# A selective scan on VectorE: an empty instruction ahead of each unit's input product takes over the scan's waits for ScalarE and GpSimd

## The chip, the cores and the metric

The kernel runs on one core of one Trainium2 chip. The metric is the device time of one execution in microseconds, and a kernel is judged by the median over its runs. All times in this document come from such runs, or from a hardware profile of one execution.

## The reference, cut to what matters

The reference is two layers, each a layer norm with a mixing block and a feed-forward block added to the residual, for 4 sequences of 256 tokens with 512 features. The change lies in the mixing block of the second layer, a selective state space scan over 1024 channels with 16 states each:

```
def step(h, inp):
    x_t, dt_t, B_t, C_t = inp
    dA = jnp.exp(dt_t[..., None] * A)
    dBx = dt_t[..., None] * B_t[:, None, :] * x_t[..., None]
    h = dA * h + dBx
    y = jnp.einsum('bdn,bn->bd', h, C_t)
    return (h, y)
...
y = (ys + D_param[None, :, None] * xc) * jax.nn.silu(z)
return jnp.einsum('bdl,hd->blh', y, out_proj_w)
```

For each channel and state there is a decay `dA`, an input product `dBx`, a recurrence over 256 time steps, and a weighted sum of the 16 states by `C`. Around it stand the input projections (`x` and `z`), a causal convolution, the small projections that give `dt`, `B` and `C`, the gate, the output projection, and a routed feed-forward block with 8 experts.

## The kernel before, in words

The first 330 us of the execution hold the first layer (attention and gated feed-forward), in which TensorE works nearly all the time. The rest is the second layer, and it is a chain of 128 **units**. A unit `u` is one sequence `b` (4), one group `c` of 128 channels (8), and one group `g` of 4 states (4): `b, c, g = u // 32, u % 32 // 4, u % 4`. Its tile is 128 partitions by 4 x 256 elements: 32 channels on each quarter of the partitions crossed with the states, and four pieces of 256 time steps side by side.

Every unit passes over four engines:

- **Decays (ScalarE, `decays`, L980).** Four exponentials of `dt * A` into one of three buffers `decay[(u - 4) % 3]`. The loop issues the decays of unit `u + 2` at the head of unit `u`, and the buffer is the one that the scan of unit `u - 1` reads, so the decays of `u + 2` wait for the scan of `u - 1`.
- **Input product (VectorE, `scan_in`, L986).** `bx = B * (dt * x)`. `dus` comes by DMA (four transfers, one for each partition quarter) for each group of four units. `bx` is one PSUM buffer, so the product of a unit waits for the scan of the unit before.
- **Scan (VectorE, `scan`, L1001).** `h = decay * h + bx` as one scan instruction over 1024 elements. `h` has two buffers, so the scan of unit `u` may not overwrite what GpSimd's product of unit `u - 2` still reads. The scan therefore waits for three engines: VectorE itself (`bx`), ScalarE (the decays of `u`) and GpSimd (`hc` of `u - 2`).
- **Weighting and sum (GpSimd L1006, TensorE L1018).** `hc = C * h` on GpSimd into one of three buffers, then four small matmuls add the states up in `ysum`.

The order of the work is written out by hand: lists of calls by unit number (`put`, `put_mid`, `put_late`, `put_end`) place the projections, convolutions, transposes, routing, gates and loads of the next sequence between the units. Each engine executes its instructions in that order. GpSimd has other work between its `hc` products (`step_out` L914 to L918, `step_x` L925, the gate L1026, the convolution's sums L811), and so does ScalarE (activations of the step sizes, table loads at L954 and L708, copies). VectorE has `bx`, the scan, and few other instructions: layer norm statistics (L720, L721, L729), the norm of the small projection (`pp_norm`, L845, issued between `bx` and the scan of one unit per sequence) and the routing (L1053 to L1085).

In the built program an instruction holds one wait of its own; what it must wait for besides stands in front of it as EventSemaphore instructions that hold up to two waits each. Before the change, an EventSemaphore with the waits for VectorE and ScalarE stands between `bx` and the scan, and the scan itself holds the wait for GpSimd. Where the wait for ScalarE is not needed, the EventSemaphore holds the one for VectorE alone. `bx` holds a wait for VectorE, with two EventSemaphores for the DMAs ahead of it in every fourth unit.

Of the kernel before, what the change touches and what calls it, by code (L numbers as in the profile page):

```python
# [11 lines left out]
AF = mybir.ActivationFunctionType  # L12
# [16 lines left out]
NG = 4  # L29
# [12 lines left out]
def block_kernel(  # L42
# [24 lines left out]
    nc = tc.nc  # L67
# [51 lines left out]
    live = {}  # L119
# [536 lines left out]
    xcs, nrms, dts, szs, crows = {}, {}, {}, {}, {}  # L656
# [15 lines left out]
    aneg = w1.tile([P, DC, NG, NU], F32, name="aneg")  # L672
# [15 lines left out]
        pads.append(t)  # L688

    decay = []  # L690

    def decay_tile(pool):
        t = pool.tile([P, NG, S], F32, name=f"decay{len(decay)}")
        nc.gpsimd.memset(t[:, :, 0:1], 0.0)
        decay.append(t)
# [268 lines left out]
    def lend(n, u):  # L964
        tag = lent[n][u]
        pool, bufs = (we, 3) if tag == "w_in" else (w1, 1)
        return pool.tile([P, NG, S], F32, tag=tag, name=n, bufs=bufs)

    def decays(u):
        b, c, g = u // PER, u % PER // NU, u % NU  # L970
        if u >= len(lent["d"]):
            da = decay[(u - 4) % 3]
        elif lent["d"][u] == "d":
            da = decay[0]
        else:
            da = lend("d", u)
            nc.gpsimd.memset(da[:, :, 0:1], 0.0)
        live["da", u] = da
        for k in range(NG):
            nc.scalar.activation(da[:, k, 1:], live["dts", b, c][:, k, 1:], AF.Exp,  # L980
                                 scale=aneg[:, c, k, g : g + 1])

    def scan_in(u):
        b, c, g = u // PER, u % PER // NU, u % NU
        bx = psx.tile([P, NG, S], F32, tag="bx", name="bx")
        nc.vector.tensor_tensor(  # L986
            bx, brow[g // 2][:, g % 2, :].unsqueeze(1).to_broadcast([P, NG, S]), live["dus", b, c], ALU.mult
        )
        live["bx"] = bx

    def scan(u, parts=1):
        b, c, g = u // PER, u % PER // NU, u % NU
        da, bx = live.pop(("da", u)), live["bx"]
        if u < len(lent["h"]):
            h, hc = lend("h", u), lend("hc", u)
        else:
            h = act.tile([P, NG, S], F32, tag="h", name="h", bufs=2)
            hc = act.tile([P, NG, S], F32, tag="hc", name="hc", bufs=3)
        for k in range(parts):
            n = slice(k * NG // parts, (k + 1) * NG // parts)  # L1000
            nc.vector.tensor_tensor_scan(  # L1001
                h[:, n].rearrange("p n t -> p (n t)"), da[:, n].rearrange("p n t -> p (n t)"),
                bx[:, n].rearrange("p n t -> p (n t)"), 0.0, ALU.mult, ALU.add,
            )

            (nc.vector if k == NG - 1 else nc.gpsimd).tensor_tensor(  # L1006
                hc[:, n], h[:, n],
                crows[b][:, g, :].unsqueeze(1).to_broadcast([P, NG // parts, S]), ALU.mult,
            )
        live["hc", u] = hc  # L1010
# [138 lines left out]
    for i in range(2):  # L1149
        v = vec[:, 6 + i, :]  # L1150
        nc.scalar.activation(px[:, i, :], px[:, i, :], AF.Identity, bias=v[:, V_CB : V_CB + 1],
                             scale=v[:, V_CW + KC - 1 : V_CW + KC])
# [33 lines left out]
    u, e, lw = live["u"], live["e"], live["lw"]  # L1186
# [21 lines left out]
    for n, t in (("dt", dt[:, 1, :]), ("du", du[:, 1, :])):  # L1208
        live[n, 0, 0] = scr.tile([2, P, S], F32, tag=n, name=f"{n}d")
        nc.sync.dma_start(live[n, 0, 0][1], t)  # L1210
    decays(0)
    scan_in(0)
    spread("dt", 0, 1)
    spread("du", 0, 1)
    b_rows(0, 1)
    c_rows(0, 1)
    decays(1)
    one_step(2)

# [157 lines left out]
    for u in range(total + 2):  # L1377
# [5 lines left out]
        if 3 <= u < total - 2:  # L1383
            decays(u + 2)
        for f, a in at.get(u, ()):
            f(*a)
        if u < total:
            if u:
                scan_in(u)
            for f, a in mid_at.get(u, ()):  # L1390
                f(*a)
        if shut == (0, 0):
            take_sum(0, 0)
        if u > total:
            b, c = shut
# [3 lines left out]
        if u < total:  # L1399
            scan(u, 1 if u < total - 1 else 4)  # L1400
            if u < 3:
                decays(u + 2)
# [11 lines left out]
        if late and u >= total - PER + 22:  # L1414
            c = late.pop(0)
# [115 lines left out]
```

## Time and profile before

| What | Value |
|---|---|
| Runs (three) | 840.86, 839.10, 839.61 us |
| Median of them | 839.61 us |
| Span of the profiled execution, first to last instruction | 839.1 us |
| VectorE busy | 655.1 us (78% of the span), 604 instructions |
| GpSimd busy | 496.7 us (59%), 389 instructions |
| ScalarE busy | 554.7 us (66%), 1124 instructions |
| TensorE busy | 748.8 us (89%) |
| Mean granted TensorE clock | 0.957 |
| VectorE busy between 466 and 550 us | 79.01 of 84 us |
| VectorE busy between 720 and 831 us | 105.87 of 111 us |

The page gives no time of the profiled execution besides its span; the median of the runs is 0.5 us longer than that span, which is taken as what lies around it.

How to read the profile: PE is TensorE, DVE is VectorE, ACT is ScalarE, POOL is GpSimd, SP issues DMAs. A row of instruction groups gives line, engine, operation, `out<-in` with shapes and the count, then busy time and mean duration of one in ns, then the engine's idle time just before these instructions and what ended it. A row of the timeline gives start and duration in us, and in brackets an idle time of 0.15 us or more ahead of it with the instruction that ended it; shorter gaps are read from the difference of start plus duration and the next start. A row of the waits gives who waited, for whom, the total, how often and the longest. EventSemaphores and empty instructions don't count as busy time.

### The profile page before, as it was taken

Reading aid. Unit: us, or ns where it says so; the run is one execution under the profiler, and the core shown is the slowest. Engines: PE = TensorE matmul, PEld = TensorE weight load, DVE = VectorE, ACT = ScalarE, POOL = GpSimd, SP = SyncE. Lnnn points to the kernel's source line nnn. Section 1 sums busy time; section 2 is a strip of 40 time slices with the busy share of each in tenths; the row PEclk is TensorE's granted clock in tenths of the full one; section 3 lists DMA queues with packets and bytes.
Section 4 is the critical chain, followed back from the end, with each engine's and each line's share of the span. In section 5 each row is a group of like instructions: output and inputs, shape, how many; then the busy total and the mean of one; then the engine's idle time right before and its main releaser. Section 6 shows DMA issues by size and latency. Waiting matters only on the chain.

```text
span 839.1 us, 11113 instructions
## 1 busy us (share of the span) xinstructions
PE 748.8 (89%) x3846; PEld 429.7 (51%) x3846; DVE 655.1 (78%) x604; ACT 554.7 (66%) x1124; POOL 496.7 (59%) x389
## 2 busy tenths in 40 slices
PE   4999999999999999999887899888999987956885
PEld 2665545666555676666543457444457444312331
DVE  4486756288634435798899999989999989999996
ACT  4335564435556277699896898687898786865561
POOL 3133332001343333688869799769699769798764
PEclk9799999999999999999999999989999989998998
DMA  7233332001222332554593554443553343343400
GB/s 226 63 101 105 97 101 62 1 1 38 76 76 80 114 57 64 151 140 125 137 215 114 150 155 125 110 103 117 144 164 114 88 113 111 103 125 102 113 26 25
DMA packets 68642, 86.71 MB, mean 103 GB/s; under 512 B 12221, under 2 KB 52169, under 8 KB 68458
## 3 DMA queue, kind: packets, MB, share of 16 engines
q1 hardware_dynamic: 58794, 65.81, 29.3%
q0 software_dynamic: 9072, 18.35, 7.9%
q10 hardware_dynamic: 720, 1.84, 0.6%
q8 instruction: 30, 0.49, 0.2%
q14 instruction: 26, 0.21, 0.1%
HBM read 66.58 MB, written 10.22 MB: 92 GB/s over the span
## 4 chain that ended last, share of the span: by engine, by line
PE 51%; DVE 25%; ACT 15%; POOL 5%; issue 3%; DMA 1%; DVEq 0%; POOLq 0%; ACTq 0%; SPq 0%
DVE h L1001 15%; ACT decay L980 7%; PE pg L444 6%; PE pu L444 5%; PE po L469 5%; PE px L757 4%; DVE bx L986 4%; POOL hc L1006 4%; PE av L397 4%; PE px L804 4%; PE ysum L1018 3%; PE scT L386 2%; DVE mpl L354 2%; PE pp L831 2%; PE po L1114 2%
## 5 line engine op out<-in xcount | busy, mean ns | idle before, releaser
L1006 POOL TENSOR_TENSOR hc<-h,cr 128x1024 f32<-128x1024 f32 (+1 forms) x130 | 301.7, 2323 | 79.9 <-DVE h L1001 67.5
L1001 DVE TENSOR_TENSOR_SCAN h<-decay,bx 128x1024 f32<-128x1024 f32 (+1 forms) x129 | 288.2, 2236 | 27.0 <-POOL hc L1006 4.7
L980 ACT ACTIVATE decay<-dts,aneg 128x255 f32<-128x255 f32 x504 | 213.4, 501 | 52.3 <-DVE h L1001 42.2
L986 DVE TENSOR_TENSOR bx<-brow,dus 128x1024 f32<-128x1024 f32 x128 | 157.7, 1232 | 5.0 <-DMA dus<-dud 0.6
L1018 PE MATMUL ysum<-hc,stack 128*32 128x256 f32 x1024 | 89.6, 419 | 42.2 <-POOL hc L1006 41.9
L456 POOL TENSOR_TENSOR hlo<-g,hhi 128x512 fp32r<-128x512 f32 x28 | 35.8, 1280 | 115.0 <-ACT hhi L455 115.0
L354 DVE TENSOR_REDUCE mpl<-sc 128x4 f32<-128x1024 f32 x64 | 76.7, 1219 | 22.8 <-PE sc L352 21.3
L427 POOL DMA_DIRECT2D wgu<-in_wgu x56 | 31.1, 555 | 95.9 <-PE pg L444 94.7
L388 ACT ACTIVATE pe<-scT 128x1024 f32<-128x1024 f32 x64 | 64.0, 1023 | 22.9 <-PE sc L352 14.3
L1114 PE MATMUL po<-ow,xc 128*128 128x512 f32 x128 | 69.4, 646 | 4.3 <-POOL xc L1026 3.9
L1018 PEld LDWEIGHTS ysum<-hc,stack 128*32 128x32 f32 x1024 | 21.3, 111 | 100.3 <-POOL hc L1006 70.6
L948 PE MATMUL pz<-xn1T,w_in 128*128 128x256 f32 x256 | 69.4, 420 | 0.0
L948 PEld LDWEIGHTS pz<-xn1T,w_in 128*128 128x128 f32 x256 | 50.8, 208 | 20.7 <-issue 11.9
L757 PE MATMUL px<-xn1T,w_in 128*128 128x256 f32 x256 | 60.9, 383 | 0.4 <-ACT sz L954 0.3
L757 PEld LDWEIGHTS px<-xn1T,w_in 128*128 128x128 f32 x256 | 47.6, 190 | 13.0 <-issue 2.5
L452 DVE SCALAR_TENSOR_TENSOR g<-g,pg 128x512 f32<-128x512 f32 x28 | 19.2, 686 | 43.1 <-ACT g L451 43.1
L444 PE MATMUL pg<-xhi,wgu 128*128 128x512 f32 x112 | 49.6, 443 | 1.0 <-ACT xhi L244 1.0
L469 PE MATMUL po<-wd,hhi 128*128 128x512 f32 x112 | 49.2, 439 | 0.0
L444 PE MATMUL pu<-xhi,wgu 128*128 128x512 f32 x112 | 47.6, 425 | 0.8 <-DVE g L454 0.8
L455 ACT CAST hhi<-g 128x512 fp32r<-128x512 f32 x28 | 17.3, 619 | 45.8 <-DVE g L454 45.8
L444 PE MATMUL pg<-xlo,wgu 128*128 128x512 f32 x112 | 44.9, 401 | 0.7 <-DVE xlo L251 0.7
L444 PE MATMUL pu<-xlo,wgu 128*128 128x512 f32 x112 | 44.5, 397 | 0.0
(237 smaller groups left out, 1276.8 us busy)
## 6 DMA issues: line engine op xcount, KB each, us to landing
dts<-dtd SPq DMA_DIRECT2D x124, 128.0 KB, 2.8
dus<-dud SPq DMA_DIRECT2D x124, 128.0 KB, 3.2
wgu<-in_wgu POOLq DMA_DIRECT2D x56, 256.0 KB, 2.7
w_in<-in_inz SPq DMA_DIRECT2D x16, 512.0 KB, 4.9
w_in<-in_inx SPq DMA_DIRECT2D x14, 512.0 KB, 4.3
dtd<-dt SPq DMA_DIRECT2D x15, 256.0 KB, 2.2
dud<-du SPq DMA_DIRECT2D x15, 256.0 KB, 2.2
wd<-in_wd POOLq DMA_DIRECT2D x7, 512.0 KB, 3.6
```

Of the source, the lines that this page charges most:

```text
L354: nc.vector.tensor_reduce(mpl2[b % 2][:, qb, 2 * hp : 2 * hp + 2, 16 + 2 * gq : 18 + 2 * gq], sc.rearrange("p i (f k) -> p i f k", f=2), A ...
L388: nc.scalar.activation(pes[b, k][:, 2 * t : 2 * t + 2, :], sc, AF.Exp)
L444: mm(ps, lhsT=wgus[i][:, hc, :], rhs=xs[j][:, hc, :], start=(hc == 0 and j == 0), stop=(hc == HC - 1 and j == 1))
L469: mm(po, lhsT=hids[th][j][:, m, i * P : (i + 1) * P], rhs=wd[:, m, :], start=False, stop=(m == MC - 1 and j == 1))
L757: mm(px[:, i, :], lhsT=w[:, i, hc, :], rhs=xns[b][:, hc, :], start=(hc == 0), stop=(hc == HC - 1))
L948: mm(pz[:, i, :], lhsT=w[:, i, hc, :], rhs=xns[b][:, hc, :], start=(hc == 0), stop=(hc == HC - 1))
L980: nc.scalar.activation(da[:, k, 1:], live["dts", b, c][:, k, 1:], AF.Exp, scale=aneg[:, c, k, g : g + 1])
L986: nc.vector.tensor_tensor(bx, brow[g // 2][:, g % 2, :].unsqueeze(1).to_broadcast([P, NG, S]), live["dus", b, c], ALU.mult)
L1001: nc.vector.tensor_tensor_scan(h[:, n].rearrange("p n t -> p (n t)"), da[:, n].rearrange("p n t -> p (n t)"), bx[:, n].rearrange("p n t -> ...
L1006: (nc.vector if k == NG - 1 else nc.gpsimd).tensor_tensor(hc[:, n], h[:, n], crows[b][:, g, :].unsqueeze(1).to_broadcast([P, NG // parts, ...
L1018: mm(ysum[k * NB : (k + 1) * NB, :], lhsT=stack, rhs=hc[:, k, :], start=False, stop=(g == NU - 1))
L1114: mm(live["po", b, i], lhsT=xcs[b][:, c, i * P : (i + 1) * P], rhs=late_w["ow"][:, c, :], start=False, stop=(c == DC - 1))
```

## The change

From unit 8 on, `scan_in` first issues `engine_nop()` on VectorE, and two dependencies are added to it by hand: on the last of the four exponentials of this unit's decays (ScalarE) and on GpSimd's product `hc` of unit `u - 2`. To name them, `decays` and `scan` keep their instructions in a dictionary.

```
+    made = {}
+    early = mybir.DependencyInfo(mybir.DependencyClass.Sync, mybir.DependencyReason.DATA)
...
+            made["da", u] = nc.scalar.activation(
+                da[:, k, 1:], live["dts", b, c][:, k, 1:], AF.Exp, scale=aneg[:, c, k, g : g + 1]
+            )
 
     def scan_in(u):
         b, c, g = u // PER, u % PER // NU, u % NU
+        if u >= 8:
+            i = nc.vector.engine_nop()
+            for n in (("da", u), ("hc", u - 2)):
+                tc.add_manual_dep(i.ins, made[n].ins.name, early, reason="the scan's waits")
         bx = psx.tile([P, NG, S], F32, tag="bx", name="bx")
         nc.vector.tensor_tensor(
...
-            (nc.vector if k == NG - 1 else nc.gpsimd).tensor_tensor(
+            made["hc", u] = (nc.vector if k == NG - 1 else nc.gpsimd).tensor_tensor(
```

In the built program this gives 120 empty instructions. Of a unit from 8 on, VectorE's queue then reads: an EventSemaphore with the wait for ScalarE, the empty instruction with the wait for GpSimd, the EventSemaphores for DMAs in every fourth unit, `bx` with the wait for VectorE, and the scan with the wait for VectorE alone. Nothing else on VectorE moves, and the order of work on the other engines is the same.

Two queues besides VectorE's differ in their waits. On ScalarE, the first exponential of 57 units now also waits for ScalarE's own earlier instruction, so that its wait for the scan stands in an EventSemaphore of its own. On GpSimd, 61 of the `hc` products also wait for GpSimd's own earlier instruction; for these the waits for VectorE and TensorE share one EventSemaphore, where before it held one wait.

More of the change, by code (lines that the diff above doesn't have):

```diff
@@ L979, in decays @@
         for k in range(NG):
-            nc.scalar.activation(da[:, k, 1:], live["dts", b, c][:, k, 1:], AF.Exp,
-                                 scale=aneg[:, c, k, g : g + 1])
+            made["da", u] = nc.scalar.activation(
+                da[:, k, 1:], live["dts", b, c][:, k, 1:], AF.Exp, scale=aneg[:, c, k, g : g + 1]
+            )
     def scan_in(u):
         b, c, g = u // PER, u % PER // NU, u % NU
+        if u >= 8:
+            i = nc.vector.engine_nop()
+            for n in (("da", u), ("hc", u - 2)):
+                tc.add_manual_dep(i.ins, made[n].ins.name, early, reason="the scan's waits")
         bx = psx.tile([P, NG, S], F32, tag="bx", name="bx")
```

## The prediction

> **What bounds the kernel now.** I read the costliest groups of the page first, then the waits, then the timeline of VectorE.
>
> ```profile
> L1006 POOL TENSOR_TENSOR hc<-h,cr 128x1024 f32<-128x1024 f32 (+1 forms) x130 | 301.7, 2323 | 79.9 <-DVE h L1001 67.5
> L1001 DVE TENSOR_TENSOR_SCAN h<-decay,bx 128x1024 f32<-128x1024 f32 (+1 forms) x129 | 288.2, 2236 | 27.0 <-POOL hc L1006 4.7
> L980 ACT ACTIVATE decay<-dts,aneg 128x255 f32<-128x255 f32 x504 | 213.4, 501 | 52.3 <-DVE h L1001 42.2
> L986 DVE TENSOR_TENSOR bx<-brow,dus 128x1024 f32<-128x1024 f32 x128 | 157.7, 1232 | 5.0 <-DMA dus<-dud 0.6
> ```
>
> Scan and product give VectorE 2.29 + 1.23 us in each of 128 units. The scan has 27 us of idle time ahead of it, the product 5; who waits for whom says how little of it is waiting for the other engines.
>
> ```profile
> POOL hc L1006 <- DVE h L1001: 67.5, 50, 5.2
> ACT decay L980 <- DVE h L1001: 42.2, 28, 2.0
> DVE h L1001 <- POOL hc L1006: 4.7, 3, 3.2
> ```
>
> GpSimd and ScalarE wait for VectorE far more than it for them, so VectorE mostly sets the pace, with TensorE taking over in places (the chain that ended last runs through TensorE around 480 to 550 us). VectorE's own rows show what the idle time is:
>
> ```profile
> 805.05 1.23 DVE L986 TENSOR_TENSOR bx<-brow,dus 128x1024 f32<-128x1024 f32 x1
> 806.41 2.29 DVE L1001 TENSOR_TENSOR_SCAN h<-decay,bx 128x1024 f32<-128x1024 f32 x1
> 808.74 1.23 DVE L986 TENSOR_TENSOR bx<-brow,dus 128x1024 f32<-128x1024 f32 x1
> 810.10 2.29 DVE L1001 TENSOR_TENSOR_SCAN h<-decay,bx 128x1024 f32<-128x1024 f32 x1
> ```
>
> From product to scan there is a gap of 806.41 - 805.05 - 1.23 = 0.13 us, from scan to product 808.74 - 806.41 - 2.29 = 0.04. The unrounded medians are 0.132 and 0.035.
>
> **What the change removes.** The scan keeps one wait, and no EventSemaphore stands between product and scan. What remains of the gap is read from other pairs. In the routing, each instruction waits for the one before alone, and reads or writes PSUM as `bx` does:
>
> ```profile
> 433.60 0.20 DVE L1054 TENSOR_TENSOR w<-ex,w 128x32 f32<-128x32 f32 x1
> 433.83 0.20 DVE L1055 TENSOR_TENSOR w<-w,cst 128x32 f32<-128x32 f32 x1
> 473.07 1.23 DVE L986 TENSOR_TENSOR bx<-brow,dus 128x1024 f32<-128x1024 f32 x1
> 474.41 2.29 DVE L1001 TENSOR_TENSOR_SCAN h<-decay,bx 128x1024 f32<-128x1024 f32 x1
> ```
>
> The gap is 0.03 with one wait (first pair), and 0.11 at this scan, whose EventSemaphore holds only VectorE's wait. So it follows the waits, and I take 0.035 for the new scan: 0.097 us less in each of 120 units, 11.6 us gross.
>
> The Trainium skill speaks against this: "VectorE: DVE Perf Modes", section "The DRAIN you can't avoid", says that a semaphore after each VectorE instruction adds nothing, since the next one waits for the pipeline anyway. Here 0.035 and 0.132 differ with the waits, so I go by the rows; by the rule the gap would stay and the sum would be that of the third rival.
>
> **What it adds.** The empty instruction's waits are mostly over while the last scan runs. Does it then take time between scan and product? Not in the trace; the nearest rows are VectorE's smallest instructions without waits:
>
> ```profile
> 0.81 0.06 DVE L87 MEMSET eps<- 128x1 f32 x1 [0.81 <-PEq L1518]
> 0.84 0.06 DVE L88 MEMSET eps<- 128x1 f32 x1
> ```
>
> They follow each other at 0.03 us. An instruction without a wait also starts before the last has ended: the statistics at 463.93 start 0.09 before the scan of 461.73 ends (464.02). Two such steps end before the product could start. Lower end: 0 (not below, as the product still waits for the scan's end). Upper end: as much as the EventSemaphore that went, 0.097. I take 0, by the nearest rows. Where the wait is not over, I count 0.065 from the releaser's end to the product: 0.035 for the hand-over and 0.03 for the step (an estimate from the two rows).
>
> The extra EventSemaphores elsewhere: the first exponential of 57 units starts 0.063 later after the scan (its hand-over from 0.034 to 0.097), the 61 GpSimd products 0.03 later (0.132 less the 0.103 of the one-wait case). Both lie where those engines wait for VectorE; they count only where the engine is then late itself.
>
> **What it moves.** The wait for decays and for `hc` of two units before now holds the product too, and behind it the scan and everything on VectorE. Before, the product (1.23) and the gap (0.13) ran under this wait. Two examples, `bx` of units 58 and 29:
>
> ```profile
> 563.10 1.23 DVE L986 TENSOR_TENSOR bx<-brow,dus 128x1024 f32<-128x1024 f32 x1
> 564.26 1.70 ACT L980 ACTIVATE decay<-dts,aneg 128x255 f32<-128x255 f32 x4
> 566.05 2.29 DVE L1001 TENSOR_TENSOR_SCAN h<-decay,bx 128x1024 f32<-128x1024 f32 x1 [1.72 <-ACT decay L980]
> 451.19 2.34 POOL L1006 TENSOR_TENSOR hc<-h,cr 128x1024 f32<-128x1024 f32 x1
> 452.99 1.23 DVE L986 TENSOR_TENSOR bx<-brow,dus 128x1024 f32<-128x1024 f32 x1
> ```
>
> At 58 the decays end at 565.96, 2.86 after the product started. At 29, `hc` of unit 27 ends at 453.53, 0.54 after. With *late* for this time and *gap* for the old one between product and scan, the scan starts later by (late + 0.065 + 1.232 + 0.035) - (1.232 + gap) = late + 0.10 - gap: 1.24 us at 58, 0.51 at 29. Call it c. I went through all units: the later of the two ends lies after the product's start in 32 of 120.
>
> The gains don't simply pay for this, since a late engine doesn't get earlier with VectorE: its queue has other work (around 453 us, `hc` and step products follow on GpSimd without idle time). So I walk through the units with s, the delay of the scan against before. Each unit lowers s by 0.097; at a late unit s is at least c plus the delay that the late engine itself carries from the scan that last released it (r).
>
> - Unit 10: decays 0.68 late, c 0.65, s 0.65. Units 13 to 19 (383 to 411 us): `hc` late by up to 4.40, old gaps up to 3.20, c at most 1.30, s 1.3. Unit 20: decays, c 1.25, s 1.25.
> - Units 21 to 28: eight gains, and scans that waited for something else anyway (gaps of 0.64 and 0.49): s 0.
> - Unit 29: c 0.51, r 0.2, s 0.7. To unit 42 about -0.1. Units 43 and 47: c 0.12, r 0.25, s 0.4. Unit 51: decays, c 0.61, r 0.3, s 0.9.
> - Unit 53: the norm at L845, between product and scan, waits for ScalarE's root behind TensorE's work (gap 1.72); s falls to TensorE's delay, about 0.3, and after four gains to -0.1.
> - Unit 58: c 1.24, r 0.3, s 1.55. Unit 61: `hc` 0.77 late, c 0.74, r 1.0, s 1.75.
> - Unit 70: decays, c 0.63, r 1.0, s 1.65. Units 75 and 79: c 0.13, r 1.65, s 1.8. Unit 83: decays, c 0.32, r 1.65, s 2.0.
> - Unit 93: `hc`, c 0.54, r 1.55, s 2.1. Unit 102: decays end 0.07 before the product starts, c -0.1, r 1.6, s 1.5.
> - Units 103 to 127: no unit is late (`hc` ends 0.4 to 1.2 before, decays 1.9 or more before), 25 gains of 0.097, 2.4 us: s -0.9.
>
> After that comes the output of the last units, which follows the scan. So 839.6 - 0.9 = 838.7 us: 11.6 us are gained gap by gap and nearly all given back.
>
> **The rivals.**
>
> *Faster: the delays don't carry over.* If GpSimd and ScalarE catch up between the late units, r is 0 and s at 102 is -0.1; 25 gains make -2.5. If the units after 58 are not late at all, s is 1.24 - 69 x 0.097 = -5.4 at the end. For it: GpSimd idles 67.5 us waiting for scans, which leaves room. Against: that idle time lies elsewhere, and an engine that waits for a scan takes over its delay. I take -2.8, 836.8 us.
>
> *Slower: the empty instruction is not hidden.* If it starts only after the scan and costs 0.03 more per unit, the gain is 0.067, s is 2.1 at 102, and the end is at 2.1 - 1.7 = +0.4. At the full 0.097 there is no gain, and only late units and stalls move s: 1.25 at 20, 0.9 at 28, 1.4 at 29, 2.1 at 51, 1.5 at 53, 2.7 at 58, 3.0 at 70, 3.45 at 102, and so it stays: +3.4, 843.0 us. It decides from 0.02 per unit on. For it: no row shows such an instruction. The skill's same page, section "Two Vector instructions with no wait between them", says that an ENGINE_NOP reaches the engine; no run here shows its price.
>
> *The change doesn't do what it says.* The gap from product to scan stays at 0.13 for another reason than the waits, and the moved waits cost what the second rival's walk has plus some hand-overs: +3.9, 843.5 us. Against it stand the 0.03 and 0.11 above.
>
> **How the numbers follow.** A measurement of this kernel can tell 0.2% (1.7 us). The forecast gets 0.42: most of it within 0.2% (0.30), 0.10 faster, 0.02 slower, as a few tenths at each late unit add up. The first rival gets 0.28, all faster. The empty instruction's price gets 0.20 (0.05 within, 0.15 slower), the gap that stays 0.10 (0.01 within, 0.09 slower). Together 0.38 faster, 0.36 same, 0.26 slower. The range goes from -4.1 (between -2.8 and -5.4 of the first rival) to +3.4 (the full price): 835.5 to 843.0. The forecast's own range is 837.3 to 840.1.
>
> **What would show it.** In the new profile the gap from product to scan should be 0.035 in every unit from 8 on, and that from scan to product 0.035 in the clean stretch from 720 us on, which gives a period of 3.59 us instead of 3.69 there. Above 0.06, the empty instruction has a price. Idle time ahead of `bx` should appear, ended by GpSimd and ScalarE: 3.3 us at unit 58, 0.9 at 29, 0.9 at 93. The prediction is wrong if the scan of unit 102 starts earlier than before (the delays don't carry over) or over 2.5 us later (the gaps don't shrink).

## The result and the profile after

| | Before | Changed |
|---|---|---|
| Median of 14 runs each | 839.28 us | 840.38 us |
| Lowest to highest | 837.79 to 843.29 us | 837.75 to 842.45 us |
| Ratio of changed to before | | 1.0012 (1.0002 to 1.0021) |
| Profiled execution | 840.86 us, span 839.1 | 840.18 us, span 838.4 |

The changed kernel is 1.0 us slower by the ratio (1.1 by the two medians), where 0.9 us less was forecast. The time lies within the stated range, but the interval of the ratio lies above 1, so the sign of the forecast was wrong. Yet the two profiled executions, read against each other, differ by -0.7 us. Which of the two readings tells the effect of the change is the question of the experiments.

The page's groups of the changed kernel (busy time, mean ns of one, then idle time ahead and who ended most of it), to be held against the four rows of before:

```profile
L1013 POOL TENSOR_TENSOR hc<-h,cr 128x1024 f32<-128x1024 f32 (+1 forms) x130 | 301.9, 2324 | 80.5 <-DVE h L1008 70.4
L1008 DVE TENSOR_TENSOR_SCAN h<-decay,bx 128x1024 f32<-128x1024 f32 (+1 forms) x129 | 288.1, 2235 | 8.5 <-PE po L469 3.6
L982 ACT ACTIVATE decay<-dts,aneg 128x255 f32<-128x255 f32 x504 | 213.6, 501 | 52.8 <-DVE h L1008 38.2
L993 DVE TENSOR_TENSOR bx<-brow,dus 128x1024 f32<-128x1024 f32 x128 | 157.7, 1232 | 24.2 <-ACT decay L982 9.3
```

The idle time ahead of the scan falls from 27.0 to 8.5 us, that ahead of the product rises from 5.0 to 24.2. The sum is 32.0 before and 32.7 after: what is gained at one line is given back at the other. The waits of the changed kernel say to whom:

```profile
DVE bx L993 <- ACT decay L982: 9.3, 8, 4.1
...
DVE bx L993 <- POOL hc L1013: 6.7, 10, 1.1
```

VectorE's timeline in the stretch without late units shows the gain:

```profile
804.92 1.23 DVE L993 TENSOR_TENSOR bx<-brow,dus 128x1024 f32<-128x1024 f32 x1
806.19 2.29 DVE L1008 TENSOR_TENSOR_SCAN h<-decay,bx 128x1024 f32<-128x1024 f32 x1
808.51 1.23 DVE L993 TENSOR_TENSOR bx<-brow,dus 128x1024 f32<-128x1024 f32 x1
809.78 2.29 DVE L1008 TENSOR_TENSOR_SCAN h<-decay,bx 128x1024 f32<-128x1024 f32 x1
812.10 1.23 DVE L993 TENSOR_TENSOR bx<-brow,dus 128x1024 f32<-128x1024 f32 x1
```

Product and scan now follow each other in both directions at 0.035 us (unrounded), and the period is 812.10 - 808.51 = 3.59 us instead of 3.69. Units 29 and 58 show the loss, in the timeline with GpSimd and ScalarE beside VectorE:

```profile
451.55 2.35 POOL L1013 TENSOR_TENSOR hc<-h,cr 128x1024 f32<-128x1024 f32 x1
453.94 1.23 DVE L993 TENSOR_TENSOR bx<-brow,dus 128x1024 f32<-128x1024 f32 x1 [0.82 <-POOL hc L1013]
...
565.33 1.70 ACT L982 ACTIVATE decay<-dts,aneg 128x255 f32<-128x255 f32 x4
567.16 1.23 DVE L993 TENSOR_TENSOR bx<-brow,dus 128x1024 f32<-128x1024 f32 x1 [4.12 <-ACT decay L982]
568.43 2.29 DVE L1008 TENSOR_TENSOR_SCAN h<-decay,bx 128x1024 f32<-128x1024 f32 x1
```

The product of unit 58 starts only after its decays have ended (565.33 + 1.70), and the scan 1.27 us after the product's start (568.43 - 567.16). Before, the product lay under this wait and the scan followed 0.09 us after the decays. The hand-over has two sizes: 0.04 us from GpSimd's end at 453.90, 0.13 from ScalarE's at 567.03. ScalarE's wait stands in an EventSemaphore ahead of the empty instruction, GpSimd's in the empty instruction itself. In every fourth unit, where the EventSemaphores for DMAs stand between the empty instruction and the product, it is 0.24 us after a late `hc` (units 44, 48, 76 and 80) and 0.33 after late decays (unit 20); the prediction had one value, 0.065.

### The profile page after: what moved, and what is told of

The parts are those of the page before. It is cut to its first block, busy times and chain, and to the rows that moved or that the text cites. A ratio compares the mean times of both kernels' runs of the same rounds, so it can differ in the third digit from the quotient of the medians.

```text
span 838.4 us, 11286 instructions
## 1 busy us (share of the span) xinstructions
PE 750.9 (90%) x3846; PEld 429.6 (51%) x3846; DVE 654.6 (78%) x604; ACT 554.2 (66%) x1124; POOL 496.9 (59%) x389
## 4 chain that ended last, share of the span: by engine, by line
PE 45%; DVE 23%; POOL 12%; ACT 9%; issue 5%; DMA 5%; SPq 1%; POOLq 0%; ACTq 0%; DVEq 0%
DVE h L1008 11%; POOL hc L1013 8%; PE pg L444 6%; DVE bx L993 6%; PE pu L444 5%; PE po L469 5%; PE av L397 4%; ACT decay L982 3%; PE po L1121 2%; PE px L759 2%; DMA dus<-dud 2%; PE scT L386 2%; DVE mpl L354 2%; PE ysum L1025 2%; DMA dts<-dtd 2%
## 5 line engine op out<-in xcount | busy, mean ns | idle before, releaser
L993 DVE TENSOR_TENSOR bx<-brow,dus 128x1024 f32<-128x1024 f32 x128 | 157.7, 1232 | 24.2 <-ACT decay L982 9.3
L1121 PE MATMUL po<-ow,xc 128*128 128x512 f32 x128 | 72.4, 671 | 5.3 <-POOL xc L1033 4.9
```

Source lines behind the costliest of these rows:

```text
L993: nc.vector.tensor_tensor(bx, brow[g // 2][:, g % 2, :].unsqueeze(1).to_broadcast([P, NG, S]), live["dus", b, c], ALU.mult)
L1121: mm(live["po", b, i], lhsT=xcs[b][:, c, i * P : (i + 1) * P], rhs=late_w["ow"][:, c, :], start=False, stop=(c == DC - 1))
```

## Experiments

The theory: the empty instruction is free and the waits between product and scan cost 0.097 us in each unit; the loss lies wholly in units whose decays or `hc` are late, because the product no longer runs under that wait. Rivals: the empty instruction has a price; or the loss comes from something else that the change brings (the extra EventSemaphores on ScalarE and GpSimd).

| Run | Kernel | Median, us | Ratio to before (95%) |
|---|---|---|---|
| e1 | before, again | 840.37 | 1.0003 (0.9988 to 1.0018) |
| e2 | changed, again | 840.98 | 1.0005 (0.9985 to 1.0024) |
| e3 | empty instruction without waits | 839.26 | 0.9986 (0.9969 to 1.0003) |
| e4 | empty instruction behind the product | 834.60 | 0.9927 (0.9899 to 0.9955) |
| e5 | none in 34 late units | 835.54 | 0.9946 (0.9933 to 0.9960) |
| e6 | only in those 34 | 844.39 | 1.0055 (1.0039 to 1.0072) |
| e7 | wait for the decays alone | 843.74 | 1.0041 (1.0026 to 1.0057) |
| e8 | wait for GpSimd alone | 839.34 | 0.9997 (0.9987 to 1.0008) |
| e9 | two empty instructions, one wait each | 840.06 | 1.0005 (0.9996 to 1.0014) |
| e10 | e4, and the like on GpSimd | 835.18 | 0.9951 (0.9938 to 0.9964) |

The ratios are to runs of before made alongside, whose medians are 839.91 us for e1 to e4, 839.52 for e5 to e8 and 839.40 for e9 and e10. A ratio can differ a little from that of the two medians: e4 is 5.3 us below before by the medians and 6.1 by the ratio. Differences below are by the ratio.

### e1 and e2: both kernels again

> The kernel before once more, for a second profile of it and for the scatter. Its profiled execution took 840.86 us (span 839.1), above the median of 839.28, and the prediction's walk was made on it. Theory (the profiled execution of before was a long one, because a TensorE-bound or DMA-bound stretch was longer in it): this profile has a span of about 837.5, ratio 1.000, and the 1.5 us lie in one or two places (the norm at unit 53 or 85, the DMA wait at unit 89), not in the late units. Rival (the profile was typical and the runs scatter evenly): span 839 and the same times unit by unit within 0.2 us.

> The changed kernel once more. Theory (gaps shrink by 11.6 us in all, the product held at the late units gives it back; net a few tenths to 1 us above before's typical execution): ratio 1.000 to 1.002, gap 0.035 in every unit. Rival (a cost outside the late units, such as the extra waits on ScalarE and GpSimd or a slower TensorE): this profile shows GpSimd's or ScalarE's queues later at units where they aren't fed by a scan.

The changed kernel was again a little above before (1.0005), now with an interval that holds no change. The gaps of e1 are those of the first profile. Its span of 838.5 us lies between the two expectations; 0.41 of the 0.6 us by which it is shorter lie at the norm of unit 53 (idle 0.91 against 1.32). Its decays differ too: those of unit 38 end 0.54 us after the start of the product, against 0.07 before it in the first profile, and at 51 the end is 0.17 after instead of 0.64. The old order hides such differences, since the product runs for 1.23 us under them; the changed order pays for each. In e2 the product is held 1.24 us at unit 38 and 0.94 at unit 102, against 0.78 and 0.42 in the first profile of the same program.

### e3: the empty instruction alone

```
         if u >= 8:
-            i = nc.vector.engine_nop()
-            for n in (("da", u), ("hc", u - 2)):
-                tc.add_manual_dep(i.ins, made[n].ins.name, early, reason="the scan's waits")
+            nc.vector.engine_nop()
```

> The 120 empty instructions at the same place, without any wait of their own; the scan keeps its three waits. Theory (the empty instruction is hidden behind the scan's end): ratio 1.000 within 0.1%, gap from scan to product 0.035 as before, from product to scan 0.132. Rival (it has a price that the change pays too): 0.03 to 0.097 us more per unit, up to +11 us where VectorE sets the pace, some +3 to +6 us in all, and the gap from scan to product is 0.06 to 0.13.

VectorE's timeline of e3 in the clean stretch:

```profile
806.23 1.23 DVE L991 TENSOR_TENSOR bx<-brow,dus 128x1024 f32<-128x1024 f32 x1
807.60 2.29 DVE L1006 TENSOR_TENSOR_SCAN h<-decay,bx 128x1024 f32<-128x1024 f32 x1
809.92 1.23 DVE L991 TENSOR_TENSOR bx<-brow,dus 128x1024 f32<-128x1024 f32 x1
```

The gap from scan to product, where the empty instruction stands, is 809.92 - 807.60 - 2.29 = 0.03, and that from product to scan 0.14 by the rounded rows (0.133 unrounded), as before. So the instruction costs nothing here: the records of the changed kernel put it at 13 ns, starting 75 ns before the scan ahead of it ends. The prediction's second rival has fallen, and what shortens the gap are the waits that it takes over, not the instruction.

### e4: the same waits, behind the product

The four lines move from `scan_in`, ahead of `bx`, to the head of `scan`, between `bx` and the scan:

```
     def scan_in(u):
...
-        if u >= 8:
-            i = nc.vector.engine_nop()
...
         bx = psx.tile([P, NG, S], F32, tag="bx", name="bx")
...
     def scan(u, parts=1):
...
+        if u >= 8:
+            i = nc.vector.engine_nop()
...
```

> The same empty instruction with the same two waits, but between product and scan instead of ahead of the product: the gap can shrink, and the product isn't held. Theory (what the change loses is the product and gap that used to run under the wait, and the gap depends on the waits alone): 4 to 7 us faster than before, -5.6 by the walk without the 1.2 us at the late units, ratio 0.992 to 0.995; scan's gap 0.035 where nothing is late. Not the full 11.6, since GpSimd, ScalarE and TensorE set the pace in places. Rival (the gap needs the waits ahead of the product, or the empty instruction behind the product costs what the EventSemaphore cost): gap 0.10 to 0.13, ratio 1.000.

```profile
L1008 DVE TENSOR_TENSOR_SCAN h<-decay,bx 128x1024 f32<-128x1024 f32 (+1 forms) x129 | 288.1, 2235 | 18.9 <-POOL hc L1013 6.0
L982 ACT ACTIVATE decay<-dts,aneg 128x255 f32<-128x255 f32 x504 | 213.2, 502 | 46.6 <-DVE h L1008 32.0
L989 DVE TENSOR_TENSOR bx<-brow,dus 128x1024 f32<-128x1024 f32 x128 | 157.7, 1232 | 5.0 <-DMA dus<-dud 0.7
```

The idle time of the two groups is 18.9 + 5.0 = 23.9 us instead of 32.0. Unit 58 in the timeline:

```profile
558.86 1.23 DVE L989 TENSOR_TENSOR bx<-brow,dus 128x1024 f32<-128x1024 f32 x1
561.09 1.70 ACT L982 ACTIVATE decay<-dts,aneg 128x255 f32<-128x255 f32 x4
562.92 2.29 DVE L1008 TENSOR_TENSOR_SCAN h<-decay,bx 128x1024 f32<-128x1024 f32 x1 [2.83 <-ACT decay L982]
```

The product runs at once, the scan starts 0.13 us after the decays, and the gap is 0.035 in units that are not late: the empty instruction runs its waits off while the product runs. The same instruction with the same two waits, and 6.1 us less than before instead of 1.0 more. The extra waits elsewhere are in this program too: in the profiles of both the changed kernel and e4, ScalarE has 231 EventSemaphores against 174 before, and 58 of the `hc` products of units 8 to 126 have the waits for VectorE and TensorE in one EventSemaphore. So neither they nor the empty instruction make the loss, and the position is left as the cause. The profiled execution is the shortest of e4's six (832.50 us) and starts its first scan 2.0 us earlier than the first profile of before (327.1 against 329.1), so its span overstates the gain. It is also the version that beats both kernels.

### e5 and e6: the late units apart from the others

One list, used in e5 as `if u >= 8 and u not in LATE`, in e6 as `if u in LATE`:

```
+    LATE = (10, *range(13, 21), 29, 30, 31, 38, 43, 44, 47, 48, 51, 58, *range(60, 64), 70, 75, 76,
+            79, 80, 83, *range(93, 97), 102)
```

> The change, but not in the 34 units where the waits are late or nearly so (10, 13 to 20, 29 to 31, 38, 43, 44, 47, 48, 51, 58, 60 to 63, 70, 75, 76, 79, 80, 83, 93 to 96, 102): these keep the old scan with three waits. Theory (86 gaps of 0.097 are gained, and nothing is given back by held products; GpSimd, ScalarE and TensorE still set the pace in places): by the walk -4.8 us, ratio 0.993 to 0.996. Rival (the loss lies in the extra waits on ScalarE and GpSimd, or in the empty instruction, and not in held products): most of the loss stays, ratio 0.999 to 1.001.

> The complement: the empty instruction with its two waits only in those 34 units. Theory: it carries the loss, +2.9 us by the walk, ratio 1.002 to 1.005, with products held as in the whole change (about 3.7 us at unit 58, 0.8 at 29 and 93). Rival: ratio 1.000 or below, since 34 gaps are shorter.

By the ratios this is -4.5 and +4.6 us. The two parts sum to about zero, which is the whole change: a gain in 86 units, given back in 34. The two groups of e6:

```profile
L1010 DVE TENSOR_TENSOR_SCAN h<-decay,bx 128x1024 f32<-128x1024 f32 (+1 forms) x129 | 288.2, 2236 | 16.4 <-PE po L469 3.6
L995 DVE TENSOR_TENSOR bx<-brow,dus 128x1024 f32<-128x1024 f32 x128 | 157.7, 1232 | 20.1 <-ACT decay L984 7.9
```

Their idle time is 16.4 + 20.1 = 36.5 us, 4.5 above the 32.0 of before, about its extra time. It was expected at +2.9, so the late units cost more than the rows of before said. Not all of the surplus need be held products: the norm of unit 53 has 1.76 us of idle time ahead of it in this profile, against 1.32 before, at a granted TensorE clock of 0.93 between 500 and 550 us, against 0.97.

### e7 and e8: which wait it is

```
-            for n in (("da", u), ("hc", u - 2)):
+            for n in (("da", u),):               # e7; in e8: (("hc", u - 2),)
```

> The empty instruction carries only the wait for the decays; the scan keeps the waits for VectorE (in an EventSemaphore) and GpSimd. The gap shrinks from 0.132 to 0.103 only, and the product is held at units 10, 20, 51, 58, 70, 83 and 102, which wait for decays. Theory: +0.9 us by the walk (0.03 gained per unit, late decays cost what they do in the change), ratio 1.000 to 1.003. Rival (GpSimd's late products cause nearly all of the loss): ratio 0.997 to 0.999.

> The empty instruction carries only the wait for GpSimd's buffer; the scan keeps the waits for VectorE (in an EventSemaphore) and ScalarE. ScalarE has no extra waits in this build. Gap 0.103; the product is held at units 13 to 19, 29, 43, 47, 61, 75, 79, 93. Theory: +0.6 us by the walk, ratio 0.999 to 1.002. Rival (the decays' waits, or the 57 extra waits on ScalarE that come with them, cause nearly all of the loss): ratio 0.997 to 0.999.

The two groups of e7, then those of e8:

```profile
L1008 DVE TENSOR_TENSOR_SCAN h<-decay,bx 128x1024 f32<-128x1024 f32 (+1 forms) x129 | 288.3, 2237 | 18.7 <-PE po L469 3.6
L993 DVE TENSOR_TENSOR bx<-brow,dus 128x1024 f32<-128x1024 f32 x128 | 157.7, 1232 | 16.3 <-ACT decay L982 12.2
```

```profile
L1008 DVE TENSOR_TENSOR_SCAN h<-decay,bx 128x1024 f32<-128x1024 f32 (+1 forms) x129 | 288.2, 2236 | 17.6 <-PE po L469 3.6
L993 DVE TENSOR_TENSOR bx<-brow,dus 128x1024 f32<-128x1024 f32 x128 | 157.7, 1232 | 16.7 <-POOL hc L1013 12.2
```

In both, one wait is left between product and scan and the gap is 0.103. With the product held for the decays alone the kernel is 3.4 us slower, nearly four times what was expected (0.9); with the product held for GpSimd alone no difference can be told. So the wait for the decays weighs more than that for `hc`. The 57 extra waits on ScalarE are in e7 and not in e8, but e4 has them too and is faster than before. How much of the 3.4 us is held products stays open: e7's profile has 2.11 us of idle time at the norm of unit 53 and a clock of 0.93 between 500 and 550 us, e8's has none there and a clock of 1.00. The idle time of the two groups is much the same in both (35.0 and 34.3), so the sums of a page do not tell these two apart. The spans (843.0 and 838.9 us) do only in part, since e8's first scan starts 2.0 us earlier (327.2 against 329.2).

### e9: the waits in two empty instructions

```
-            i = nc.vector.engine_nop()
             for n in (("da", u), ("hc", u - 2)):
+                i = nc.vector.engine_nop()
                 tc.add_manual_dep(i.ins, made[n].ins.name, early, reason="the scan's waits")
```

> The changed kernel with two empty instructions ahead of the product instead of one, each with one of the two waits, so that no EventSemaphore stands ahead of them. In the changed kernel's profile the product starts 0.13 us after late decays end and 0.04 after a late hc. Theory (the 0.13 is the EventSemaphore with ScalarE's wait and the empty instruction behind it, one after the other): 0.05 to 0.08 after late decays, 0.04 after hc; 0.06 us less at some eight units, so the time stays within 0.1% of the change, ratio to before 0.999 to 1.002. Rival (ScalarE's semaphore itself is slow to arrive, or a second empty instruction costs its own step): 0.13 stays, or the gap from scan to product grows above 0.035.

Unit 58 in the timeline of e9:

```profile
563.27 1.70 ACT L982 ACTIVATE decay<-dts,aneg 128x255 f32<-128x255 f32 x4
565.01 1.23 DVE L993 TENSOR_TENSOR bx<-brow,dus 128x1024 f32<-128x1024 f32 x1 [4.12 <-ACT decay L982]
```

The hand-over from the late decays falls from 0.13 to 565.01 - 563.27 - 1.70 = 0.04 (0.047 unrounded): a wait in the empty instruction itself hands over faster than one in the EventSemaphore ahead of it. It happens at eight or so units, too few to show in the time.

### e10: e4, and an empty instruction on GpSimd

```
+            if u >= 8 and k == 0:
+                i = nc.gpsimd.engine_nop()
+                tc.add_manual_dep(i.ins, made["ys", u - 3].ins.name, early, reason="hc's buffer")
             made["hc", u] = (nc.vector if k == NG - 1 else nc.gpsimd).tensor_tensor(
...
```

> The empty instruction between product and scan, and the same on GpSimd: an empty GpSimd instruction ahead of hc carries its wait for TensorE (hc's buffer), so that hc keeps the wait for the scan alone. Theory (waits that lie in EventSemaphores on the path cost about 0.06 us at each hand-over): hc starts 0.08 after its scan instead of 0.14, and GpSimd's busy stretches get 0.06 shorter a unit; 0.5 to 2 us less than with VectorE's alone, ratio to before 0.989 to 0.993. Rival (GpSimd's hand-over is its own, or its empty instruction costs more than it saves): ratio 0.993 or above.

The ratio is in the rival's range. From the scan's end to `hc` it is 0.147 us in 49 units, against 0.170 in e4 and 0.145 before. But in these units `hc` does not keep the wait for the scan: it holds a wait for GpSimd's own earlier instruction, and the wait for VectorE stands in an EventSemaphore behind the empty instruction. In six units (25, 26, 70 and 89 among them) `hc` does hold VectorE's wait and starts right behind its scan, and there the hand-over is 0.08. Units 22 and 26:

```profile
422.64 2.29 DVE L1008 TENSOR_TENSOR_SCAN h<-decay,bx 128x1024 f32<-128x1024 f32 x1
425.07 2.38 POOL L1016 TENSOR_TENSOR hc<-h,cr 128x1024 f32<-128x1024 f32 x1 [1.23 <-DVE m L1071]
441.80 2.29 DVE L1008 TENSOR_TENSOR_SCAN h<-decay,bx 128x1024 f32<-128x1024 f32 x1
444.16 2.35 POOL L1016 TENSOR_TENSOR hc<-h,cr 128x1024 f32<-128x1024 f32 x1
```

So the size that was expected is there where the wait is where it was meant to be; the program as built had it there too seldom to test the theory by its time, which is that of e4 or a little more.

### Which reading tells the effect: more profiles by stages

One more run of before (e11) was 843.27 us:

> A third profile of the kernel before. In the first, the decays of unit 38 end 0.07 us before their product starts, in the second 0.54 after it; either way the scan starts on time, since product and gap (1.36 us) run under the wait. Theory (the end of the decays against the product moves by some tenths of a us from one execution to the next, and the old order hides it): again another value at units 38, 51, 58, 70, 83, 102, with the gap ahead of the scan at 0.132 wherever the decays are less than 1.3 us late. Rival (the profiled execution was typical of these units): the same values within 0.1 us.

The theory held in part: at 38 the decays now end 0.20 us before the start of the product, at 70 0.18 before it instead of 0.66 after, at 83 0.84 after instead of 0.35, while 58 and 102 are as before to 0.01 us. So single executions of one program differ by more than the change does. Four more profiles were taken and read in three stages: the start of the first scan (nothing that the change touches lies before it), scan 0 to 28, and scan 28 to 127.

> The kernel before, unchanged, for its stages: start of the first scan, scan 0 to scan 28, scan 28 to scan 127. Three executions of it so far: 329.1 / 121.5 / 377.9, 329.1 / 121.5 / 377.3, 327.2 / 125.4 / 378.4 us. Theory 1 (the new order pays for decays whose lateness differs from execution to execution): the last stage stays within 377.2 to 378.5 here, while that of the changed kernel varies by several us. Theory 2 (the traces of before show no execution of the median length, and the difference lies in the first stages): an execution with a start near 327.2 and a second stage near 121.5 turns up, with a span near 837.

> The changed kernel, unchanged, for the same stages. Two executions so far: 329.1 / 122.8 / 376.9 and 327.4 / 122.8 / 381.3 us. Theory 1: second stage 122.8 again, last stage anywhere between 376 and 382, on average 1 to 2 us above that of before. Theory 2: the last stage is at or below before's 377.3 to 378.4.

> As the first of these: the kernel before; theory 1 has its last stage within 377.2 to 378.5 us; theory 2 has a start near 327.2 with a second stage near 121.5.

> As the second of these: the changed kernel; theory 1 has its last stage between 376 and 382 us with an average above before's, theory 2 at or below 377.3 to 378.4.

| Execution | Run, us | First scan starts | Scan 0 to 28 | Scan 28 to 127 |
|---|---|---|---|---|
| before, first profile | 840.86 | 329.1 | 121.5 | 377.9 |
| before, e1 | 840.23 | 329.0 | 121.5 | 377.3 |
| before, e11 | 843.27 | 327.2 | 125.4 | 378.4 |
| before, s1 | 840.42 | 329.1 | 121.5 | 377.4 |
| before, s3 | 839.10 | 327.7 | 121.5 | 377.4 |
| changed, first profile | 840.18 | 329.1 | 121.7 | 376.9 |
| changed, e2 | 841.62 | 327.4 | 121.7 | 380.0 |
| changed, s2 | 840.43 | 329.3 | 121.7 | 376.9 |
| changed, s4 | 840.47 | 329.3 | 121.7 | 376.9 |

The expectation for s2 quotes 122.8 us for the second stage and 381.3 for e2's last; the right values are those of the table, 121.7 and 380.0. The second theory holds in these four runs, but not in e2: in three executions of the changed kernel in four the last stage is 0.5 us shorter than before, and the second stage always 0.2 longer, so typically the change makes the scans 0.3 us shorter. The first theory expected the last stage of the changed kernel to be longer on average; both means are 377.7. s3, near the median of before, is an execution whose first scan starts 1.4 us earlier with the same scans behind it. So the first profile of before was a late start, and the medians differ by which starts and which rare long executions fall into the runs. Two of the executions with an early start pay in the scans: e11 most of all in units 9 to 28, e2 in units 38 to 102.

## Why the prediction was right and wrong

**The gap (right).** 0.035 in every unit from 8 on was forecast, and 3.59 us of period; both are measured. The gap is 0.035, 0.103 and 0.132 with no wait, one and two in front of the scan, which always holds one wait itself (changed, e7 or e8, before). So the prediction's third rival has fallen. The Trainium skill, "VectorE: DVE Perf Modes", section "The DRAIN you can't avoid", measured that one semaphore after each instruction costs nothing extra. That does not carry over to the further waits here, which cost 0.068 and 0.097 us. The extra EventSemaphores on the other engines were sized rightly too: hand-overs from the scan of 0.095 us on ScalarE and 0.170 on GpSimd, where 0.097 and about 0.175 were expected.

**The empty instruction at 0 (right).** e3 shows it by itself.

**The late units (right in kind).** 3.3 us of idle time ahead of `bx` were expected at unit 58, 0.9 at 29 and 0.9 at 93; 4.12, 0.82 and 0.81 were measured in the first profile. e4, e5 and e6 show that the loss comes with the products held there. The table below shows that the delays carry over (2.10 us are left at unit 102), so the prediction's first rival has fallen too.

**The step that failed: the late decays at units 38 and 58, and TensorE's delay between them (mis-sized).** s, the delay of the scan against before, counted from the first scan, for s2 against s1, two executions that start within 0.2 us of each other:

| Unit | 10 | 20 | 28 | 29 | 38 | 42 | 51 | 57 | 58 | 61 | 70 | 83 | 93 | 102 | 127 |
|---|---|---|---|---|---|---|---|---|---|---|---|---|---|---|---|
| predicted | 0.65 | 1.25 | 0 | 0.7 | none | -0.1 | 0.9 | -0.1 | 1.55 | 1.75 | 1.65 | 2.0 | 2.1 | 1.5 | -0.9 |
| measured | 0.74 | 1.54 | 0.20 | 0.87 | 0.90 | 0.50 | 1.12 | 0.44 | 2.80 | 2.96 | 2.46 | 2.83 | 2.53 | 2.10 | -0.31 |

The walk holds to 0.3 us up to unit 29, and the last 25 units give back 2.41 (2.4 forecast). What failed are the terms of the late decays at two units, and the 0.3 us taken as TensorE's delay at the norm of unit 53: it is 0.40 in the first profiles, but 0.84 in s2 against s1. At 38 the walk has no term, since the decays were read as 0.07 us early, from a profile in which they were; in e1, s1 and s3 they are 0.54, 0.54 and 0.43 late. At 58, c + r was taken as 1.24 + 0.3, but ScalarE starts these decays 1.07 us later than before (565.33 against 564.26 in the first profiles), so r was 1.07, and 1.24 + 1.07 = 2.3 is what those two profiles have (2.38). In s2 against s1, each counted from its first scan, r is 1.50, and 2.74 of the 2.80 in the table. Of the delay in the first profiles, 0.78 is there at the copy of `cr` some eight microseconds earlier on ScalarE's queue, which waits for TensorE (556.75 against 555.97), and 0.39 is idle time ahead of the step sizes' L888 that before does not have; together they are 0.10 more than the 1.07, and this much is made up on the way. The hand-over was another 0.07 short for decays (0.134 against the 0.065 taken) and 0.02 too long for `hc` (0.041). Altogether the scans end at -0.3 where -0.9 was forecast. The pair of first profiles has -0.8 (-0.77), close to the forecast, but partly by luck: with r at 58 three and a half times what was taken, it comes out only because the delay then falls from 2.4 at unit 58 to 2.0 at 93, where the walk had it grow from 1.55 to 2.1.

**The base (wrong).** The prediction took 0.5 us as what lies around the span, from the median of three runs. It is 1.8 us in every run that has both numbers (840.18 to 838.4, for one). The profiled execution of before was thus the run of 840.86 us, 1.6 above the median of 839.28. The forecast set the walk of a long execution off against the median. This makes the 838.7 us too low, but does not by itself turn the sign of the difference.

**What stays open.** The scans end 0.3 us earlier in a typical execution, and the medians say 1.0 us more (0.4 in e2's comparison). Of those 1.3 us, none is in the scans of three traces in four; the fourth, e2, has +2.8 there. The mean granted TensorE clock, which is on record for nearly every run, narrows this down. In the comparison that e2 belongs to:

| Runs | Clock 0.951 or less | Clock above 0.951 |
|---|---|---|
| before, 29 | 12: eight of 839.1 to 839.9 us, four of 843.1 to 843.5 | 17, median 840.2 us |
| changed, 12 | 7: 840.8 to 842.7 us | 5, median 838.0 us |

Of the changed kernel's 14 runs in the result, the six at 0.951 or less take 840.7 to 842.5 us, the other eight at most 840.6. So what the medians have above the typical trace lies mostly in executions at the lower clock, and e2 (0.949) is the changed kernel's only profile of one. Its scans end 3.1 us later than those of s2, and 1.2 of these arise at once, at the norm of unit 53, which e2 and s2 show as

```profile
546.02 0.48 DVE L847 SCALAR_TENSOR_TENSOR nrm<-pp,lnw,rs 64x256 f32<-64x256 f32 x1 [1.98 <-ACT rs L715]
546.28 0.48 DVE L847 SCALAR_TENSOR_TENSOR nrm<-pp,lnw,rs 64x256 f32<-64x256 f32 x1 [0.74 <-ACT rs L715]
```

Between 500 and 550 us the granted clock is 0.93 in e2 and 0.97 in s2. The rest arises at units 38 and 70 (0.4 each), 86 to 89 (0.9) and 102 (0.5), with 0.4 given back at 58. The walk took 0.3 us as TensorE's delay at this norm; in e2 against s1 it is 2.4. Whether the change brings these executions about is not shown: it would need the stages of many runs. e1, the same program as before, also had its median at 840.37, so a start that is late more often need not have to do with the change at all.

## What to carry to other kernels

A wait moved ahead of work that used to run under it must be priced at each unit where it is late, not by its average; put the empty instruction that carries it directly ahead of the instruction that needs it, and the shorter gap comes without most of the loss (-6.1 us here). Lateness read from one execution of a program whose old order hides it is not to be trusted to a few tenths of a microsecond: bound it by several profiles. And before a forecast of a tenth of a per cent is made, match the profiled execution to one of the runs, by its span and what lies around it.

## What the runs showed of the hardware

The gap between product and scan on VectorE follows the waits in front of the scan: 0.035, 0.103 and 0.132 us for none, one and two in an EventSemaphore. An empty instruction with no open wait is recorded at 13 to 14 ns and runs off before the instruction ahead of it has ended (e3). A wait that ends last hands over in 0.04 to 0.05 us when an empty instruction ahead of the product holds it and in 0.13 when it stands in an EventSemaphore ahead of the empty instruction (unit 58 in e9 and in the changed kernel). On GpSimd the hand-over from the scan to `hc` is 0.08 us where `hc` holds the wait itself (six units of e10), 0.145 with an EventSemaphore of one wait ahead (before) and 0.170 with one of two waits (changed). In the profiles of before, of the changed kernel, e3 and e6 to e9, the idle time at the norm of unit 53 goes with the TensorE clock granted between 500 and 550 us: none at 1.00 (e3, e8), 0.7 to 1.4 us at 0.97, 1.8 to 2.1 at 0.93 (e2, e6, e7). In e4, e5 and e10, where VectorE comes to this norm earlier, it is 2.0 to 3.2 us. An earlier first scan need not help: in e11 it starts 2.0 us earlier than in the first profile, and scan 28 starts 1.8 us later (452.5 against 450.7).
